# The length-1 step of a recurrent layer: gates as seven half-size products in place of eight

## The chip, the cores and the metric

The kernel runs on one core of a Trainium2 chip. The metric is device time in microseconds (us), the median over runs. Engines are named as in the profile: PE is TensorE's matmul, PEld its weight load, DVE is VectorE, ACT is ScalarE, POOL is GpSimd, SP is SyncE, which here issues DMAs. "L1368" is line 1368 of the kernel before. Each engine works through a queue of its own, in order, and waits on semaphores for the others.

## The reference

Four residual layers over `x` of 128 x 64 x 256, each followed by a layer norm. The change is in the fourth. It makes `h` with two graph convolutions and then runs four small LSTMs over `h`, with windows of 1, 2, 3 and 4 steps, each writing back the last step of each window:

```python
h = relu(einsum('ts,bsh->bth', adj, x @ Wg0 + bg0))
h = relu(einsum('ts,bsh->bth', adj, h @ Wg1 + bg1))
for p in range(1, MAX_SKIP + 1):
    nw = Tv // p
    wins = h[:, :nw * p, :].reshape(Bv * nw, p, Hd)
    last = lstm_last(Wih[p - 1], Whh[p - 1], bih[p - 1], bhh[p - 1], wins)
    idx = arange(nw) * p + (p - 1)
    h = h.at[:, idx, :].set(last.reshape(Bv, nw, Hd))
```

For a window of one step the state is zero, so the f gate and `Whh` drop out:

```python
i, g, o = sigmoid(x Wi + bi), tanh(x Wg + bg), sigmoid(x Wo + bo)
h = o * tanh(i * g)
```

Each of x Wi, x Wg, x Wo is a product of rows of 256 with a 256 x 256 matrix, in float32.

## The kernel before

The layer works on four pairs (`pair` 0 to 3) of 32 batches. `Hs[pair]` holds `h` transposed: 128 partitions of features, then two halves `n` of 16 batches, two feature blocks `k`, 64 time steps, 16 batches. The loop `lstm(pair)` runs lengths 1 to 4 one after another and yields after each unit of work; units 0 to 7 are length 1, 8 to 21 length 2, 22 to 32 length 3, 33 to 47 length 4. At those yields side steps are run, as `put(pair, part, *units)` has entered them by hand: `gcn` (the graph convolutions that make the next pair's `h`; eleven steps each: load, two fetches, two norms, neighbours, and so on), `final` (residual, norm and output of what is finished, in two steps), and `prepare` (load of a length's weights; at the first use also the sums of weight blocks on POOL, L1198).

Everything in the loop is issued through `given` (L110), which puts each instruction behind the latest one of PE, DVE, ACT and POOL, so that the order of an engine's queue is the order of the program. Waits come from the data: reading what was written, and overwriting what is still to be read, PSUM banks and SBUF tiles alike.

Length 1 before: for each half n and each run of 32 time steps (512 columns) and each output block j of 128, three gates i, g, o with two products each (L1368), so 8 units of 6 products, 48 in a pair. ACT evaluates each gate out of its PSUM bank (L1372), DVE multiplies i and g (L1373), ACT takes tanh (L1374), DVE multiplies by o into `h` (L1379). There are six banks for this ring (`lbank`).

Lengths 2 to 4 make their later steps with seven products of 128 x 128 blocks in place of eight (class `Gate`), with sums of weight blocks (`S`) and of input columns (`xsums`, `hsums`). Each product has a bank of its own. The class `Seven` of the third layer (L796) does the same in three banks and accumulates a second product into a bank that was copied out.

The weights of lengths 2 to 4 live in two rotating pairs of tiles, `wx` (8 x 512 per partition) and `wh` (7 x 512). The weights of length 3 take the tiles that length 4 of the pair before has used. Their load is step `prepare(weights_of[k, 3])` at unit 0.

Of the kernel before, what the change touches and what calls it, by code (L numbers as in the profile page):

```python
# [17 lines left out]
P = 128  # L18
NB = 128
N = 64  # L20
# [21 lines left out]
def kernel(ctx: ExitStack, tc: tile.TileContext, i, out):  # L42
# [1125 lines left out]
    class Weights:  # L1168
# [7 lines left out]
        def load(self):  # L1176

            x = we.tile([P, 8, 2 * D], F32, name="wx", bufs=2)
            h = we.tile([P, 7, 2 * D], F32, name="wh", bufs=2)
            self.tiles = x, h  # L1180
            raw = [t[:, :4].rearrange("p k c -> p (k c)").rearrange("p (k c) -> p k c", k=KD) for t in (x, h)]
            if self.p in self.ready:
                for t, d in zip(self.tiles, self.ready[self.p]):
                    nc.sync.dma_start(t, d)
            else:
                for t, w in zip(raw, (i["WihT"], i["WhhT"])):
                    nc.sync.dma_start(t, w[self.p - 1].rearrange("(k p) c -> p k c", p=P))
            self.raw = [t.rearrange("p k (g m c) -> p k g m c", g=4, m=2) for t in raw]
            sums = [[t[:, j].rearrange("p (g c) -> p g c", g=4) for j in range(4, t.shape[1])] for t in (x, h)]

            self.S = [sums[0], [self.raw[1][:, 0, :, 1]] + sums[1]]
# [156 lines left out]

    def lstm(pair):
# [4 lines left out]


        for n in range(2):
            for w0 in range(0, N, QT // GB):
                Hw = H[:, n, :, w0:w0 + QT // GB, :]
                ends = []

                def gates(j):
                    i_, g_ = (late.tile([P, QT // GB, GB], F32, name="gate", bufs=6) for _ in range(2))
                    o = late.tile([P, QT // GB, GB], F32, name=("hid", "hs")[j], bufs=1)
                    banks = [lbank([QT // GB, GB]) for _ in range(3)]
                    for b, name in zip(banks, "igo"):
                        mw = {"i": 0, "g": 2, "o": 4}[name] + j
                        for k in range(KD):
                            nc.tensor.matmul(b, wih1[:, k, mw * P:(mw + 1) * P], Hw[:, k],  # L1368
                                             start=k == 0, stop=k == KD - 1)
                    for b, name, dst in zip(banks, "igo", (i_, g_, o)):  # L1370
                        at, f = gate_of(name)
                        nc.scalar.activation(dst, b, f, bias=bias[:, 0, 2 * at + j:2 * at + j + 1])  # L1372
                    nc.vector.tensor_mul(i_, i_, g_)  # L1373
                    nc.scalar.activation(g_, i_, AF.Tanh)  # L1374
                    ends.append((o, g_))
                    if j == KD - 1:

                        for jj, (o, t) in enumerate(ends):
                            nc.vector.tensor_mul(Hw[:, jj], o, t)  # L1379

                for j in range(KD):
                    given(gates, j)
                    yield "at", unit
                    unit += 1

        for p in range(2, SKIP + 1):
# [80 lines left out]
            def late_columns(r):  # L1467

                if pair < NP - 1 or p == 2 or r:
                    return [slice(0, nw)], []  # L1470
                mine, q = range(nw), p - 1
                wrote = [w for w in mine if w * p % q == q - 1 and w * p < N // q * q and (q > 2 or w * p >= N // 2)]
                step = wrote[1] - wrote[0]
                assert wrote == list(range(wrote[0], nw, step))[:len(wrote)]
                if wrote[0] < step:
                    return [slice(n, nw, step) for n in range(step) if n != wrote[0]], [slice(wrote[0], nw, step)]
                return [slice(0, wrote[0])], [slice(wrote[0], nw)]

            def begin(n, r, ms, parts):
# [3 lines left out]
                for m in ms:  # L1483
                    if (n, m) not in begun:
                        begun[n, m] = lbank([2, nw, GB]) if joint else [lbank([nw, GB]) for g in range(2)]
                    for g in range(1 if joint else 2):
                        for c in parts:
                            for k in range(KD):
                                x = inp(r, 0, k)
                                b, x = (begun[n, m][:, :, c], x[:, :, c]) if joint else (begun[n, m][g][:, c], x[:, g, c])  # L1490
                                nc.tensor.matmul(b, w.raw[0][:, k, at, m, :], x, start=k == 0, stop=k == KD - 1)  # L1491
# [210 lines left out]
    first = [prepare(weights_of[0, p]) for p in (2, 3)]  # L1702
    for n in [0, 0, 0, 1, 1, 0, 1, 0, 0, 1, 0, 0, 1, 1, 0, 2, 1, 3, 1, 1, 2, 2, 3, 3]:
        given(next, parts[n])
    for part in first:
        next(part)
# [13 lines left out]
    put(0, first[1], 9, 11)  # L1720
# [7 lines left out]
    for k in range(NP):  # L1728
        if k:
            put(k, prepare(weights_of[k, 3]), 0)  # L1730
# [3 lines left out]
        for n in range(2):  # L1734
# [4 lines left out]
            if k < NP - 1:  # L1739
                put(k + 1, final(g, SKIP - 1), n, n + 2)  # L1740
        if k < NP - 1:
            put(k, prepare(weights_of[k + 1, 2]), 34)
            for n, keys in enumerate([
                    [0, 2, 3, 5, 6, 9, gap(11), 12, wait(15), 16, gap(18)],
                    [2, 5, 6, 8, 9, 19, wait(22), gap(22), gap(25), 26, gap(29)],
                    [6, 8, 9, 12, 13, 27, wait(33), gap(33), gap(36), 37, 38],
                    [9, 11, 12, 15, 16, 34, gap(40), 41, gap(44), 45, 46]]):
# [49 lines left out]
```

## Time and profile before

| what | us |
|---|---|
| median of three runs (2048.69 to 2051.10) | 2050.42 |
| profiled execution | 2053.11 |
| its span, first to last instruction | 2050.9 |
| length 1 of pair 0 (with the last steps of the first `h`) | 798.4 to 861.9 |
| length 1 of pair 1 | 1132.7 to 1173.9 |
| length 1 of pair 2, first and last start of a product | 1444.5 to 1485.3 |
| length 1 of pair 3, first and last start of a product | 1756.4 to 1797.1 |

In a group of instructions the columns are: line, engine, operation, output <- inputs, shapes, count, then busy us and mean ns of one, then idle time of the engine just before and who ended it. In a table of windows: the window, its length, busy us and instruction count of PE, PEld, DVE, ACT and POOL, the clock that was granted to PE (1.00 is full), the share of the DMA engines and GB/s. In a timeline: start, length, engine, line, operation, count of merged instructions, and in brackets the idle time before. A float32 product shows as two records.

### The profile page before, as it was taken

To read this page: it belongs to the slowest core of one execution; us is meant where nothing else is said; L and a number is where in the kernel's file an instruction comes from. 1 tells how busy PE (TensorE), PEld (TensorE's weight loads), DVE (VectorE), ACT (ScalarE), POOL (GpSimd) and SP (SyncE) were. 2 spreads that over 40 slices of the span, in tenths; PEclk is the share of its full clock that TensorE was granted. 3 is DMA by queue.
4 is the path that set the end of the run, shared out by engine and by line. 5 is a ranking of instruction groups with operands and counts; after the bars stand their busy time and mean duration, and the time that the engine had idled before them with its cause. 6 is when DMAs were issued, how large, how long until landed. Compare 5 with 4: busy or idle time off the path is not lost.

```text
span 2050.9 us, 31078 instructions
## 1 busy us (share of the span) xinstructions
PE 1959.1 (96%) x11391; PEld 1329.2 (65%) x11391; DVE 1185.8 (58%) x2683; ACT 968.4 (47%) x1852; POOL 809.7 (39%) x961
## 2 busy tenths in 40 slices
PE   5999999999899999999999999999999999999996
PEld 4666667766454445577678477677567667568685
DVE  7456665564457456574466674456674457544566
ACT  2766667666334633544343644343544333543333
POOL 1123334343345535263445253345243335224264
PEclk8999999999999998999999999999999999999998
DMA  5344442332112026351232532032532022401022
GB/s 137 74 66 68 79 69 54 66 49 40 31 35 60 26 97 242 124 180 52 88 139 63 185 114 93 11 128 72 169 101 83 1 109 70 141 0 77 1 65 69
DMA packets 235959, 170.66 MB, mean 83 GB/s; under 512 B 150560, under 2 KB 213536, under 8 KB 232480
## 3 DMA queue, kind: packets, MB, share of 16 engines
q1 hardware_dynamic: 233952, 166.72, 28.7%
q8 instruction: 90, 1.47, 0.3%
q0 software_dynamic: 1024, 1.05, 0.2%
q10 hardware_dynamic: 832, 0.92, 0.1%
q14 instruction: 61, 0.50, 0.1%
HBM read 107.82 MB, written 60.82 MB: 82 GB/s over the span
## 4 chain that ended last, share of the span: by engine, by line
PE 74%; DVE 13%; POOL 4%; ACT 4%; issue 3%; DMA 2%; SPq 1%; POOLq 0%; ACTq 0%; DVEq 0%
PE l L1535 27%; PE l L1491 9%; PE l L1368 8%; PE pz L820 4%; PE e L346 3%; PE pz L749 3%; PE m L318 3%; PE g L1331 2%; PE pz L1017 2%; PE m L321 2%; PE z L355 2%; PE m L253 2%; PE m L436 1%; PE g L1319 1%; DVE ln_st L95 1%
## 5 line engine op out<-in xcount | busy, mean ns | idle before, releaser
L1535 PE MATMUL l<-xs,wx 128*128 128x256 f32 (+1 forms) x896 | 276.8, 399 | 5.0 <-DVE gate L1554 4.0
L1535 PE MATMUL l<-hs,wh 128*128 128x256 f32 (+1 forms) x896 | 275.1, 399 | 3.1 <-DVE hs L1405 3.1
L86 POOL TENSOR_TENSOR ln_rs<-ln_rs,mhalf 128x2 f32<-128x2 f32 (+2 forms) x98 | 84.3, 860 | 448.9 <-DVE ln_rs L98 442.9
L1550 ACT ACTIVATE kept<-l 128x256 f32<-128x256 f32 (+1 forms) x224 | 88.6, 403 | 339.7 <-PE l L1535 338.4
L1535 PE MATMUL l<-H,wx 128*128 128x256 f32 (+1 forms) x672 | 210.2, 401 | 3.4 <-DVE gate L1563 3.4
L1535 PE MATMUL l<-hid,wh 128*128 128x256 f32 (+1 forms) x672 | 208.8, 399 | 0.0
L1535 PEld LDWEIGHTS l<-xs,wx 128*128 128x128 f32 x896 | 168.8, 190 | 49.3 <-POOL st L100 4.1
L1535 PEld LDWEIGHTS l<-hs,wh 128*128 128x128 f32 x896 | 169.3, 190 | 45.5 <-DVE hs L1405 5.7
L1568 ACT ACTIVATE gate<-gate,bias 128x512 f32<-128x512 f32 (+1 forms) x280 | 170.6, 657 | 37.4 <-DVE gate L1559 31.1
L1491 PE MATMUL l<-H,wx 128*128 128x512 f32 (+4 forms) x576 | 183.7, 475 | 2.2 <-DVE H L1441 2.2
L1368 PE MATMUL l<-H,wih 128*128 128x512 f32 x384 | 167.4, 596 | 0.0
L357 ACT ACTIVATE u<-z 128x1024 f32<-128x1024 f32 x128 | 130.4, 1025 | 64.3 <-PE z L355 63.2
L1535 PEld LDWEIGHTS l<-H,wx 128*128 128x128 f32 x672 | 125.9, 190 | 42.8 <-issue 7.4
L1491 PEld LDWEIGHTS l<-H,wx 128*128 128x128 f32 x576 | 100.9, 190 | 76.2 <-issue 53.6
L1535 PEld LDWEIGHTS l<-hid,wh 128*128 128x128 f32 x672 | 127.2, 190 | 32.0 <-issue 2.6
L1368 PEld LDWEIGHTS l<-H,wih 128*128 128x128 f32 x384 | 73.2, 191 | 90.1 <-issue 83.1
L1558 POOL TENSOR_TENSOR gate<-gate,kept 128x256 f32<-128x256 f32 (+1 forms) x84 | 65.2, 776 | 158.6 <-DVE kept L1556 158.6
L329 DVE TENSOR_TENSOR qs<-m,qs 64x256 fp32r<-64x256 f32 x128 | 54.0, 422 | 109.9 <-ACT qs L328 107.8
L1409 POOL TENSOR_TENSOR hs<-hid 128x256 f32<-128x256 f32 (+1 forms) x28 | 25.5, 909 | 192.3 <-DVE hid L1438 98.6
L355 PE MATMUL z<-gath_r,qs 128*128 128x512 f32 x256 | 100.8, 482 | 0.1
L1463 ACT ACTIVATE gate<-cell 128x512 f32<-128x512 f32 (+1 forms) x88 | 58.6, 666 | 81.7 <-DVE cell L1455 59.5
L1552 DVE TENSOR_TENSOR gate<-l,kept 128x256 f32<-128x256 f32 (+1 forms) x112 | 49.1, 438 | 72.0 <-ACT gate L1568 44.1
(336 smaller groups left out, 3825.9 us busy)
## 6 DMA issues: line engine op xcount, KB each, us to landing
wx<-sums SPq DMA_DIRECT2D x9, 2048.0 KB
wh<-sums SPq DMA_DIRECT2D x9, 1792.0 KB
way<-st SPq DMA_DIRECT2D x54, 256.0 KB
st<-way SPq DMA_DIRECT2D x216, 64.0 KB
xin<-in_x SPq DMA_DIRECT2D x16, 512.0 KB
ld<-table SPq DMA_DIRECT2D x16, 512.0 KB
x_dram<-y SPq DMA_DIRECT2D x16, 512.0 KB
x2r<-x_dram SPq DMA_DIRECT2D x32, 256.0 KB
```

Of the source, the lines that this page charges most:

```text
L86: nc.gpsimd.tensor_tensor(dst, dst, mhalf[:, :n], OP.pow)
L318: nc.tensor.matmul(pq, xT[:, k, c * P:(c + 1) * P], wq[:, k, :], start=k == 0, stop=k == KD - 1)
L346: nc.tensor.matmul(pes[S][n * CG:(n + 1) * CG, :], apad[:, k, CG - HEADS - r0:2 * CG - HEADS - r0], u[:, k, :], start=r0 == 0 and k == 0, ...
L355: nc.tensor.matmul(z[:, k, :], L1[q]["qs"][c][:, s, k * P:(k + 1) * P], gath_r, start=True, stop=True)
L357: nc.scalar.activation(u, z, AF.Relu)
L820: nc.tensor.matmul(self.bank[at], lhs, rhs, start=first and n == 0, stop=n == len(self.terms) - 1, skip_group_check=True)
L1368: nc.tensor.matmul(b, wih1[:, k, mw * P:(mw + 1) * P], Hw[:, k], start=k == 0, stop=k == KD - 1)
L1491: nc.tensor.matmul(b, w.raw[0][:, k, at, m, :], x, start=k == 0, stop=k == KD - 1)
L1535: nc.tensor.matmul(self.banks[j], lhs, rhs, start=src == 0, stop=src == 1)
L1550: nc.scalar.activation(self.keep(j), b, AF.Copy)
L1558: e.tensor_tensor(t[0][:, 1], t[0][:, 1], k[5], OP.add)
L1568: given(lambda: nc.scalar.activation(dst, dst, f, bias=b))
```

## The change

For each half n the three gates g, i, o are now made whole, in this order: 256 output rows in two blocks m, 1024 columns in two halves v of 512. Weight and input are cut into 2 x 2 blocks and the product is made with seven block products (`Wide`, `seven`) in three banks: products 1 and 2 share one, 6, 7 and 4 another, 5 and 3 the third. ACT copies products 1 and 5 out, DVE adds 6, 3, 7 and 4 to what has been kept, POOL makes one more sum; the gate's functions then work in place, three of four out of SBUF. Product 4 and most of a gate's functions and multiplies (`tail`) are issued between the products of the next gate. The first g of each pair, and in pair 0 both g, are still made with eight products (`eight`).

The sums of input columns (`column_sums`, four POOL operations of 512 for each n) and the sums of weights (`Sx`), two buffers for copies (`firsts`) and half of i's result (`spare`) lie in the tiles of the weights of length 3, which `room` reserves and `load` fills later. The weight sums are computed once (`first_sums`, POOL, ahead of pair 0), stored, and fetched by DMA in later pairs. `column_sums(1)` is issued at the start of n=1 in pair 0, and after gate i of n=0 in the others.

Length 2 begins with products of half n=0 alone for g and, in part, i (`late_columns`, `begin`), ahead of those of n=1.

Side steps: the load of length 3's weights goes from unit 0 to 8 (pair 0: load 8, sums 13 and 15, from a load ahead of the loop and sums at 9 and 11); the last finals from n and n+2 to 9+n and 12+n; the loads, fetches and norms of three of the four `gcn` parts to later units. The numbering of units is kept: g, i, o of n=0 are units 0, 1, 2, unit 3 follows at once; likewise 4 to 7.

```diff
+    def first_sums():
+        S = rooms_of(0)[1]
...
+        for dst, x, y, op in ((2, a11, a21, OP.subtract), (0, a21, a22, OP.add), (1, S[:, 0], a11, OP.subtract),
+                              (3, a12, S[:, 1], OP.subtract)):
+            nc.gpsimd.tensor_tensor(S[:, dst], x, y, op)
+        d = dram.tile([P, 3 * QT], F32, name="sums1")
+        nc.sync.dma_start(d, S.rearrange("p j g c -> p (j g c)"))
+        sums_kept.append(d)
...
+        Tn, Sx, firsts, spare = rooms_of(pair)
+        if pair:
+            nc.sync.dma_start(Sx.rearrange("p j g c -> p (j g c)"), sums_kept[0])
...
+        def column_sums(n):
+            T, e = Tn[n], nc.gpsimd
+            e.tensor_tensor(T[:, 0], half(n, 0, 1), half(n, 0, 0), OP.subtract)
+            e.tensor_tensor(T[:, 1], half(n, 1, 1), T[:, 0], OP.subtract)
+            e.tensor_tensor(T[:, 2], half(n, 1, 1), half(n, 0, 1), OP.subtract)
+            e.tensor_tensor(T[:, 3], half(n, 1, 0), T[:, 1], OP.subtract)
...
+            def product(self, j):
+                b = given(self.multiply, j)
+                t, add = self.t, nc.vector.tensor_add
+                if j == 1:
+                    given(nc.scalar.activation, self.first, b, AF.Copy)
+                elif j == 5:
+                    given(nc.scalar.activation, t[1][1], b, AF.Copy)
+                elif j == 2:
+                    self.act(0, 0, b)
+                elif j == 6:
+                    given(add, t[0][1], b, self.first)
+                elif j == 3:
+                    given(add, t[0][1], b, t[0][1])
+                elif j == 7:
+                    given(add, t[1][0], b, self.first)
+                    given(nc.gpsimd.tensor_tensor, t[1][1], t[1][0], t[1][1], OP.add)
+                else:
+                    given(add, t[1][0], b, self.first)
...
+            def after(self, m, v):
+                if self.name == "i":
+                    g = self.gates["g"][m][v]
+                    if m:
+                        given(nc.gpsimd.tensor_tensor, self.t[m][v], self.t[m][v], g, OP.mult)
+                    else:
+                        given(nc.vector.tensor_mul, self.t[m][v], self.t[m][v], g)
+                    given(nc.scalar.activation, self.t[m][v], self.t[m][v], AF.Tanh)
+                elif self.name == "o":
+                    given(nc.vector.tensor_mul, half(self.n, m, v), self.t[m][v], self.gates["i"][m][v])
+
+            def tail(self):
+                self.act(0, 1)
+                yield
+                self.after(0, 0)
+                self.after(0, 1)
+                yield
+                self.product(4)
+                self.act(1, 1)
+                yield
+                self.act(1, 0)
+                yield
+                self.after(1, 1)
+                self.after(1, 0)
+
+            def last(self):
+                self.act(0, 1)
+                self.product(4)
+                self.after(0, 0)
+                self.act(1, 0)
+                self.after(1, 0)
+                self.act(1, 1)
+                self.after(0, 1)
+                self.after(1, 1)
...
+        def seven(G, rest, order):
+            G.product(order[0])
+            next(rest, None)
+            G.product(order[1])
+            next(rest, None)
+            G.product(order[2])
+            next(rest, None)
+            G.product(order[3])
+            next(rest, None)
+            for _ in rest:
+                pass
+            for j in order[4:]:
+                G.product(j)
+
+        rest = iter(())
         for n in range(2):
...
+            if n == 0:
+                given(column_sums, 0)
+            elif pair == 0:
+                given(column_sums, 1)
+            gates = {}
+            for name in "gio":
+                G = Wide(name, n, gates)
+                if name == "g" and (n == 0 or pair == 0):
+                    eight(G, rest)
+                    rest = iter(())
+                else:
+                    seven(G, rest, (1, 6, 5, 2, 7, 3) if (n, name) == (1, "o") else (1, 6, 5, 2, 3, 7))
+                    rest = G.tail()
+                if (n, name) == (1, "o"):
+                    G.last()
+                elif name == "i" and n == 0 and pair:
+                    given(column_sums, 1)
+                yield "at", unit
+                unit += 1
+            yield "at", unit
+            unit += 1
...
+                if p == 2 and r == 0:
+                    return [(slice(0, 1), every)], [(slice(1, 2), every)]
...
-    for part in first:
-        next(part)
+    given(first_sums)
+    next(first[0])
...
-    put(0, first[1], 9, 11)
+    put(0, first[1], 8, 13, 15)
...
-            put(k, prepare(weights_of[k, 3]), 0)
+            put(k, prepare(weights_of[k, 3]), 8)
...
-                put(k + 1, final(g, SKIP - 1), n, n + 2)
+                put(k + 1, final(g, SKIP - 1), 9 + n, 12 + n)
...
-                    [0, 2, 3, 5, 6, 9, gap(11), 12, wait(15), 16, gap(18)],
-                    [2, 5, 6, 8, 9, 19, wait(22), gap(22), gap(25), 26, gap(29)],
-                    [6, 8, 9, 12, 13, 27, wait(33), gap(33), gap(36), 37, 38],
-                    [9, 11, 12, 15, 16, 34, gap(40), 41, gap(44), 45, 46]]):
+                    [0, 1, 3, 5, 7, 9, gap(11), 12, wait(15), 16, gap(18)],
+                    [5, 9, 11, 13, 15, 19, wait(22), gap(22), gap(25), 26, gap(29)],
+                    [13, 17, 19, 21, 23, 27, wait(33), gap(33), gap(36), 37, 38],
+                    [21, 24, 26, 28, 30, 34, gap(40), 41, gap(44), 45, 46]]):
```

## The prediction

> Forecast: **slower by about 7.6 us**. The profiled execution took 2053.1 us (span 2050.9 and 2.2 around it) and would become 2060.7; the median shown, 2050.4, lies 2.7 below that execution, and I move it by the same sum: **2058.0 us**. About 0.2%, 4.1 us, is what can be told from no change.
>
> **What bounds the kernel now.** First the page's busy line, then windows over the stages of length 1 (one for each of four pairs), then TensorE's lines in order of time.
>
> ```profile
> PE 1959.1 (96%) x11391; PEld 1329.2 (65%) x11391; DVE 1185.8 (58%) x2683; ACT 968.4 (47%) x1852; POOL 809.7 (39%) x961
> ...
> 798.00:862.00 64.00, 62.20 (x406) 32.60 (x405) 33.70 (x72) 29.71 (x47) 24.65 (x29) 0.97 0.42 149
> ...
> 1132.50:1174.00 41.50, 41.50 (x99) 18.52 (x98) 24.64 (x59) 24.72 (x42) 9.96 (x15) 1.00 0.59 198
> ...
> L1368 PE MATMUL l<-H,wih 128*128 128x512 f32 x384 | 167.4, 596 | 0.0
> ...
> 1132.71 41.36 PE L1368 MATMUL l<-H,wih 128*128 128x512 f32 x96
> ```
>
> In the second pair's stage PE is busy for 41.50 of 41.50 us with nothing but L1368. A product is two records, so 384 records are 192 products: 167.4/192 = 0.872 us each, and 48 of them are the 41.4 us run. The other three engines have room. So products removed are time won, and every wait that PE newly has is time lost. In pair 0 the last norms of the first H run beside the stage:
>
> ```profile
> 806.88 1.10 POOL L100 TENSOR_SCALAR A<-x2r,ln_rs 128x256 f32<-128x256 f32 x2
> 807.94 5.18 POOL L1198 TENSOR_TENSOR wx<-wx 128x512 f32<-128x512 f32 x4
> 813.08 6.50 POOL L1198 TENSOR_TENSOR wh<-wh 128x512 f32<-128x512 f32 x4
> ...
> 807.50 1.24 PE L1249 MATMUL l<-bdT,A 64*64 64x64 f32 x32 [1.43 <-POOL A L100]
> 808.67 6.70 PE L1368 MATMUL l<-H,wih 128*128 128x512 f32 x12
> ...
> 815.01 1.76 DVE L1379 TENSOR_TENSOR H<-hid,gate 128x512 f32<-128x512 f32 x1
> 816.70 1.75 DVE L1379 TENSOR_TENSOR H<-hs,gate 128x512 f32<-128x512 f32 x1
> 818.37 1.27 DVE L1321 TENSOR_TENSOR hT<-g,rb 128x512 f32<-128x512 f32 x2
> ...
> 808.00:810.00 2.00, 1.97 (x18) 1.33 (x19) 0.69 (x1) 0.60 (x1) 2.00 (x2) 0.50 0.30 98
> ```
>
> Two things to see: POOL is occupied until 808.0, and after PE's gaps there its clock is 0.50 and six products take 6.70 us where they take 5.3.
>
> **The skill.** The Trainium skill (GPSIMD Engine Reference, 1. Specifications) says that GpSimd shares its SBUF interfaces with VectorE and contends with DVE instructions that have two SBUF inputs. The rows above agree: L1379 (two SBUF inputs) takes 1.76 beside L1198 where it takes 0.69 elsewhere, and the four POOL sums 6.50 instead of 5.18; L1321, with one input from PSUM, keeps its 0.64 each. I take 1.76 for such a multiply, and 0.65 more on POOL for each. Second, TensorE: Matmul & The Clock Gate (Part 1) puts the slow clock after an idle window of about 3.4 us. Here it came after less (0.52 us busy of 806 to 808). I go by the trace: 1.4 us lost after such a gap.
>
> **Prices.** From rows of this trace, end to end: ACT gate from PSUM 0.69 (L1372), Copy from PSUM 0.60 (L830), gate in place 0.66 (L1568), tanh 0.63 (L1374); the next one starts about 0.1 before such an end. DVE add with one PSUM input 0.69 (L832), two-SBUF multiply 0.69 alone. POOL sum of 128x512 1.27 (L116). A product can be read about 0.17 after its issue slot (its records last 0.59, issued every 0.44).
>
> **What is removed.** Per pair there are six gates (two halves n; g, i, o) of eight products. Seven of eight are made in four gates of pair 0 and five of each later pair: 19 products, 19 x 0.872 = **-16.6 us** (3.5, 4.4, 4.4, 4.4).
>
> **Pairs 1 to 3, start.** First g is eight products, 7.0 us. Beside it POOL makes the column sums, four times 1.27, and the 0.79 MB of weight sums comes by DMA; wx<-sums moves 350 to 390 GB/s, so some 2.3 us and about 2 us to start. Product 6 of i needs them at 7.9. Hidden by 2 us or more; nothing charged.
>
> **Gate o of n=0 and g of n=1.** Clock: o's product 1 starts at 0; PE's order is 1, 6, 5, i's 4, 2, 3, 7, each 0.87. ACT's order is copy 1, i's act, tanh, tanh, copy 5, i's act, o's act, i's act, tanh, tanh: ten operations, about 6.1 us, in a gate of 6.1 us. Product 3 accumulates into the bank of product 5, so it waits for copy 5, and that stands behind two tanhs whose multiplies stand on DVE behind the add of product 6.
> - Add 6: 1.95 to 2.6. POOL has i's last add 0.9 to 2.2, then column_sums(1), so both multiplies contend: to 4.3 and 5.95. Second tanh to 6.6, copy 5 to 7.15. Product 3 would have started at 4.36: wait **2.8**.
> - The other two multiplies of i are on POOL behind column_sums(1): sums 5.16 plus 1.3 of contention end at 8.6, multiplies at 9.9 and 11.2, last tanh 11.85. In pairs 1 and 2 the two scales of the moved fetch (unit 3) follow, 1.0; then copy 1 of g, to 13.35. g's product 2, which needs that bank, would start at 8.9+3.5 = 12.4: wait **1.0**, and product 3 waits **0.2** for its copy. In pair 3 (no fetch) copy 1 ends at 12.35: 0.0 and 0.2.
> - Sum 4.0 in pairs 1 and 2, 3.0 in pair 3. Contention moves waits between the two gates more than it changes the sum: without any it is about 2.5 and 1.6.
>
> **Gate i of n=1**: ACT has six operations; no wait.
>
> **Gate o of n=1.** Unit 5 puts a norm (DVE 1.9 us, as at 1165.4 to 1167.3) ahead of its add 6 in pairs 0 to 2. Copy 5 then ends at 5.7; product 3 is last here and due at 5.2: **0.5**. Pair 3: 0.
>
> **End of stage.** Before, length 2 began with windows that the last unit did not write, so PE had no wait (L1491 follows at once). Now its first products need the half just written. Covers: the g and i products of half n=0, six of 0.43 = 2.6 us. The chain: i's last two POOL multiplies end about 8.2 after o's start, tanh 8.85, act 9.4, act 10.0, multiply 10.7; PE has products until 7.0 and cover to 9.6: **1.15**, with the norm 1.35.
>
> **Pair 0.** first_sums (four sums of 384 elements, about 1.0 each between the 336-wide at 0.90 and the 512-wide at 1.27) queue on POOL behind the norms, 808.0 to 812.0; the first two column sums end at 814.6. PE: g to 805.4, the neighbour products to 808.5 (waiting about 0.9 for POOL, as before), i's product 1 to 809.4, product 6 waits to 814.6: **5.2**, and the clock gap **1.4**. o of n=0, with no column sums beside it: **0.8** to 1.0. Then g of n=1 follows the H writes of the parts directly (before, six products of n=0 stood between: PE 836.24, H written to 837.4): **1.2**. o and the end: 0.5 and 1.35. New waits 10.6 with the 0.9 that stay about 11.5; before, this stage lost 1.8 to waits and 1.4 to the clock. 11.5 - 3.2 - 3.5 = **+4.8**.
>
> **Moved steps.** Length-3 weights go from unit 0 to 8 (their 3.8 MB kept the queues over 0.8 busy from 1133 to 1148; first needed at unit 22), so SP's queue is freer early; finals to 9 to 13, norms and fetches to 9 to 30, with their way DMAs behind that load but three units ahead of their use. Finals at 12 and 13 add DVE blocks of 2.6 us to a stage with PE waits of 2.6 us in all, per pair, over lengths 2 to 4. Bounds -2 and +2 per pair; I take 0. The halved beginning of length 2 makes twice the records at half the columns: 0. A tanh that comes first could need another table load, 1.28 (L1372's), hidden in g: 0.
>
> **Sum.** Pair 0 +4.8; pairs 1 and 2: 4.0+0.5+1.35 = 5.85 less 4.36, +1.5 each; pair 3: 3.0+1.15 less 4.36, -0.2. Total **+7.6**.
>
> **Rivals.**
> - *The waits just eat the gain*, within 0.2%: there is no contention and the fetch's scales run earlier (o and g of pairs 1 to 3 at 2.5, 2.5 and 1.6: -4.4) and the pair 0 wait is 2 to 3 us shorter. +1, 2051. For: ACT is free before o. Against: the 1.76 rows.
> - *Faster*: PE does not wait for the chain from POOL's multiplies through tanh to ACT's copies. It decides at copy 1 of g ending before 9.6 after o's start (mine: 13.35). Then the waits of o and g go in all pairs (4.0, 4.0, 3.0, 0.8: -4.2 in all), and those at the ends, which stand behind the same multiplies, too (5.2): -9.4, 2041. For: POOL is busy for 24% of the stage before. Against: POOL takes its queue in order, and the program puts the column sums first.
> - *More than forecast*: each wait over 2 us also drops the clock, 1.4 in three pairs, and the DVE blocks of unit 12 and 13 cost their bound, 4 over pairs 1 and 2: +16, 2066. For: the 0.50 clock after a short gap. Against: 1.2 us waits late in the kernel left it at 1.00.
>
> **Numbers.** Forecast 0.53, within 0.2% 0.21, faster 0.16, more than forecast 0.10. Faster 0.16, same 0.21, slower 0.63. The likeliest case's own range is 2054.5 to 2063; the range 2045 to 2067 leaves out most of the faster case and the outer part of the last.
>
> **What would show it.** 43 or 44 products of 512 in each stage. PE waits for an ACT copy at product 3 of each o of n=0 and, in pairs 1 and 2, at product 2 of the next g; for POOL column sums once, about 5 us, near 809; for the H multiply at the start of length 2, about 1.2 us each. Stages of about 43 us in pairs 1 and 2, against 41.5. Wrong if PE stays at 100% there, if the wait near 809 is missing, or if lengths 2 to 4 change by more than 2 us per pair.

## The result and the profile after

The changed kernel takes 2067.28 us, median of four runs (2063.85 to 2069.47), against 2050.62 for the kernel before (2048.69 to 2051.10): a ratio of 1.0082, interval 1.0064 to 1.0099. It is slower by 16.7 us where 7.6 were forecast, and 0.3 us beyond the top of the range. The sign, the places of the new waits and most of their lengths came as forecast; their sum did not.

The profiled execution took 2069.47 us (span 2067.7), 2.2 above its median. The one shown of before was 2.5 above this median, and at least that much lies ahead of length 1: its first product of length 1 starts at 798.4, that of the trace after at 793.7, and its clock was 0.90 in the first 100 us, where the trace after has 0.93. From the first product of length 1 to the end of the span, where none of that counts, the two traces have 1252.5 and 1274.0 us. So the forecast's +7.6 stands against +21.5 of this one execution. By stages, from the start times of the products:

| stage | before | after | difference |
|---|---|---|---|
| pair 0, length 1 | 63.7 | 70.2 | +6.5 |
| pair 0, length 2 | 83.1 | 86.6 | +3.5 |
| pair 1, length 1 | 41.2 | 42.2 | +1.0 |
| pair 1, length 2 | 83.1 | 85.3 | +2.2 |
| pair 2, lengths 1 and 2 | 124.3 | 126.8 | +2.5 |
| pair 3, length 1 to the start of length 3 | 110.1 | 114.5 | +4.4 |
| length 3 of pairs 0, 1 and 2 | 262.3 | 264.0 | +1.7 |
| all the rest | 484.7 | 484.4 | -0.3 |

The page's busy line, and those rows of TensorE's waits of the changed kernel that the kernel before does not have (waited for; us in total, times, longest us). L1437 is a product of the seven, L1500 of the eight, L1659 the first step of length 2, L116 the helper through which `Wide` issues its functions, sums and multiplies.

```profile
PE 1950.8 (94%) x11449; PEld 1338.6 (65%) x11449; DVE 1236.3 (60%) x2743; ACT 987.1 (48%) x1890; POOL 902.0 (44%) x1032
...
PE l L1437 <- ACT gate L116: 10.6, 7, 2.5
PE l L1437 <- POOL wx L1392: 6.2, 1, 6.2
PE l L1659 <- DVE H L116: 5.9, 8, 1.2
PE l L1500 <- ACT H L1348: 1.3, 1, 1.3
PE l L1703 <- ACT gate L1673: 0.8, 1, 0.8
PE l L1437 <- ACT wh L116: 0.5, 1, 0.5
```

By the page TensorE is busy for 8.3 us less, but 6.1 of that lie ahead of length 1. From the first product of length 1 on it is busy for 2.2 us less (1221.2 for 1223.3), where 19 products fewer are worth 19 x 0.858 = 16.3 (a product starts every 41.2/48 = 0.858 us in a full stream of the kernel before; the prediction's 0.872 has the half clock of pair 0 and the ends of its runs of products in it). So 14 us of the saving are gone in busy time: products at half clock are longer, and so, as shown further down, are the products beside a wait. The other three engines carry 50, 19 and 92 us more. TensorE has 25.3 us of waits that it did not have, and 1.6 fewer behind POOL in pair 0: 25.3 - 1.6 - 2.2 = 21.5. The timelines show where. Pair 0 first:

```profile
803.24 1.12 PE L1437 MATMUL l<-H,wih 128*128 128x512 f32 x2
810.57 3.78 PE L1437 MATMUL l<-wx,wh 128*128 128x512 f32 x4 [6.20 <-POOL wx L1392]
814.14 1.92 PE L1437 MATMUL l<-H,wih 128*128 128x512 f32 x2
815.84 1.44 PE L1437 MATMUL l<-H,wh 128*128 128x512 f32 x2
...
831.11 1.13 PE L1437 MATMUL l<-H,wh 128*128 128x512 f32 x2 [1.80 <-ACT gate L116]
```

Then gate o of n=0 in pair 1, its end of stage, the same gate in pair 2, and the start of length 2 in pair 3:

```profile
1154.35 1.02 PE L1437 MATMUL l<-H,wih 128*128 128x512 f32 x2
1157.87 1.97 PE L1437 MATMUL l<-H,wh 128*128 128x512 f32 x2 [2.50 <-ACT gate L116]
1159.64 1.92 PE L1437 MATMUL l<-wx,wh 128*128 128x512 f32 x2
1161.34 1.07 PE L1437 MATMUL l<-H,wih 128*128 128x512 f32 x2
...
1179.16 1.13 PE L1437 MATMUL l<-H,wh 128*128 128x512 f32 x2 [0.45 <-ACT gate L116]
...
1184.91 0.70 PE L1659 MATMUL l<-H,wx 128*128 128x256 f32 x2 [1.17 <-DVE H L116]
...
1469.91 1.02 PE L1437 MATMUL l<-H,wih 128*128 128x512 f32 x2
1473.43 1.13 PE L1437 MATMUL l<-H,wh 128*128 128x512 f32 x2 [2.50 <-ACT gate L116]
1474.39 1.02 PE L1437 MATMUL l<-wx,wh 128*128 128x512 f32 x2
1475.25 1.02 PE L1437 MATMUL l<-H,wih 128*128 128x512 f32 x2
...
1814.50 0.70 PE L1659 MATMUL l<-H,wx 128*128 128x256 f32 x2 [1.01 <-DVE H L116]
1815.86 6.49 PE L1659 MATMUL l<-H,wx 128*128 128x256 f32 x21 [0.65 <-DVE H L116]
```

Product 3 of o waits 2.50 for the copy of product 5 in each of pairs 1 to 3 (forecast 2.8), product 3 of the last o waits 0.45 in pairs 0 to 2 (0.5), and at the start of length 2 TensorE waits 1.17 and 0.24 in pairs 0 to 2 (1.35 in all) and 1.01 and 0.65 in pair 3 (1.15). The first of the surprises is beside it. Products 3 and 7 take 1.97 and 1.92 in pair 1 and 1.13 and 1.02 in pair 2 after the very same wait of 2.50. The windows show a different clock (columns as in the tables of windows before: the clock granted is the third number from the end); the last two rows are pair 2's:

```profile
810.00:812.00 2.00, 1.44 (x2) 0.84 (x3) 0.00 (x0) 0.00 (x0) 1.78 (x2) 0.50 0.94 351
1158.00:1160.00 2.00, 2.00 (x3) 0.94 (x4) 0.12 (x1) 1.61 (x3) 2.00 (x2) 0.50 0.00 0
1790.00:1792.00 2.00, 2.00 (x3) 0.67 (x2) 0.69 (x2) 0.71 (x2) 2.00 (x3) 0.50 0.00 0
1818.00:1820.00 2.00, 2.00 (x6) 1.56 (x6) 0.00 (x0) 1.03 (x2) 0.82 (x2) 0.50 0.78 186
...
1472.00:1474.00 2.00, 0.57 (x2) 0.34 (x3) 0.83 (x2) 1.74 (x4) 1.92 (x2) 1.00 0.22 65
1474.00:1476.00 2.00, 2.00 (x6) 0.91 (x5) 1.24 (x2) 1.21 (x3) 2.00 (x3) 1.00 0.00 0
```

The clock was halved within the long wait of pair 0 and behind the wait in pairs 1 and 3, and once more at the start of length 2 in pair 3, behind the waits of 1.01 and 0.65. In pair 2 it was not.

### The profile page after: what moved, and what is told of

Same layout as the page of the kernel before. It is cut to its first block, busy times and chain, and to the rows that moved or that the text cites. A ratio compares the mean times of both kernels' runs of the same rounds, so it can differ in the third digit from the quotient of the medians.

```text
span 2067.7 us, 31491 instructions
## 1 busy us (share of the span) xinstructions
PE 1950.8 (94%) x11449; PEld 1338.6 (65%) x11449; DVE 1236.3 (60%) x2743; ACT 987.1 (48%) x1890; POOL 902.0 (44%) x1032
## 3 DMA queue, kind: packets, MB, share of 16 engines
q0 software_dynamic: 1024, 1.05, 0.2%
## 4 chain that ended last, share of the span: by engine, by line
PE 67%; DVE 16%; POOL 6%; ACT 5%; issue 3%; DMA 1%; SPq 1%; DVEq 0%; ACTq 0%; POOLq 0%
PE l L1703 26%; PE l L1659 8%; PE pz L820 4%; PE l L1437 4%; PE pz L749 3%; PE e L346 2%; PE m L318 2%; PE g L1336 2%; PE pz L1017 2%; PE m L321 2%; PE z L355 2%; DVE ln_st L95 2%; PE m L253 1%; PE g L1324 1%; PE l L1500 1%
## 5 line engine op out<-in xcount | busy, mean ns | idle before, releaser
L1659 PE MATMUL l<-H,wx 128*128 128x256 f32 (+5 forms) x672 | 187.8, 435 | 8.5 <-DVE H L116 5.9
L1659 PEld LDWEIGHTS l<-H,wx 128*128 128x128 f32 x672 | 119.7, 192 | 70.7 <-issue 34.4
L1703 PEld LDWEIGHTS l<-H,wx 128*128 128x128 f32 x672 | 125.8, 190 | 42.5 <-DVE gate L1731 7.4
L1613 POOL TENSOR_TENSOR cell<-gate,cell 128x512 f32<-128x512 f32 (+1 forms) x56 | 75.5, 1368 | 28.4 <-ACT gate L1736 28.4
L1731 DVE TENSOR_TENSOR gate<-l,gate 128x256 f32<-128x256 f32 (+1 forms) x112 | 50.0, 446 | 61.4 <-POOL gate L1726 35.1
```

Source lines behind the costliest of these rows:

```text
L1613: nc.gpsimd.tensor_tensor(c, t, c, OP.mult)
L1703: nc.tensor.matmul(self.banks[j], lhs, rhs, start=src == 0, stop=src == 1)
```

## The experiments

Four kernels take one cause each out of the changed kernel, one puts the moved steps alone into the kernel before, two join the repairs, one tests an order on POOL. Each was timed beside the kernel before, on the same chip.

**The weight sums of pair 0.** They are issued ahead of the last four steps of the first norms (`at` counts these steps):

```diff
...
+        if at == 20:
+            given(first_sums)
         given(next, parts[n])
-    given(first_sums)
```

> The weight sums are issued on POOL ahead of the last four norms of the first H instead of behind them; nothing else is moved. Theory A (the order of POOL's queue makes the 6.2 us wait of PE before product 6 of i in pair 0, and that gap halves PE's clock for some 5 us, a loss of about 3): the column sums start when the norms end (802.8 in the changed kernel) in place of 806.8, so the wait shrinks from 6.2 to about 2.3, and the clock loss from 3 to between 0 and 1.5; in all 5.5 to 7 us less, a median of about 2061. Theory B (the wait is for something else, such as the memory of the tiles or H): the wait stays and less than 1 us is won. If only the gap counts and the slow clock has another cause, 3.9 are won.

Measured 2063.42 us (2061.98 to 2064.61), ratio 1.0058 (1.0042 to 1.0075).

```profile
PE l L1437 <- POOL wx L1392: 2.1, 1, 2.1
```

The wait falls from 6.2 to 2.1, and the stage from 70.2 to 64.9. By the ratios about 5 us are won, somewhat less than the 5.5 to 7 expected, and the intervals of the two kernels overlap: it is the trace that decides. So it was the queue on POOL (norms, weight sums, column sums, in that order), as the prediction had it.

**The column sums of n=1, in pairs 1 to 3.**

```diff
             if n == 0:
                 given(column_sums, 0)
+                if pair:
+                    given(column_sums, 1)
...
-                elif name == "i" and n == 0 and pair:
-                    given(column_sums, 1)
```

> In pairs 1 to 3 the column sums of n=1 are issued right behind those of n=0, at the start of the stage, so that they are off POOL before gate o of n=0. Theory A (in these pairs the wait before product 3 of o and the one before product 2 of g come from POOL's column sums: they contend with DVE's two multiplies and stand ahead of POOL's multiplies): the 2.5 us wait before product 3 falls to about 0.7, there is no wait and no slow clock behind it; 3.6, 2.7 and 3.6 us less in the three pairs, about 10 in all, a median of about 2057. Theory B (ACT's queue of ten operations sets both waits, contention moves nothing): the wait stays above 2 us and less than 2 us are won in all. The waits of about 1.4 at the start of length 2 stay in both.

Measured 2059.65 us (2058.97 to 2062.33), ratio 1.0045 (1.0029 to 1.0062): by the ratios 7.6 us, the largest single repair, where about 10 were expected.

```profile
PE l L1437 <- ACT gate L116: 5.0, 7, 1.8
```

The 2.50 us waits are gone from all three pairs, and the clock stays at 1.00 there; lengths 1 and 2 gain 3.1, 2.5 and 5.3 us. The chain behind the waits can be read on the engines in pair 1 of the changed kernel, which are VectorE's two multiplies of i, POOL's column sums beside them, and the copy on ScalarE that comes last:

```profile
1153.51 3.16 DVE L116 TENSOR_TENSOR cell<-cell,hid 128x512 f32<-128x512 f32 x2
...
1154.41 1.71 POOL L1393 TENSOR_TENSOR wx<-H 128x512 f32<-128x512 f32 x1
1156.08 1.72 POOL L1392 TENSOR_TENSOR wx<-H,wx 128x512 f32<-128x512 f32 x1
...
1156.70 0.63 ACT L116 ACTIVATE cell<-cell 128x512 f32<-128x512 f32 x1 [1.05 <-DVE cell L116]
1157.24 0.58 ACT L116 ACTIVATE gate<-l 128x512 f32<-128x512 f32 x1
```

Two multiplies of two SBUF inputs take 3.16 beside the sums. Alone, two take 1.28 in this trace. The second tanh waits for them, the copy of product 5 (`gate<-l`) stands behind the tanh in ScalarE's queue, and product 3 waits for the copy.

**The copies ahead of i's tanhs.**

```diff
                 self.act(0, 1)
                 yield
-                self.after(0, 0)
-                self.after(0, 1)
                 yield
                 self.product(4)
                 self.act(1, 1)
                 yield
                 self.act(1, 0)
+                self.after(0, 0)
+                self.after(0, 1)
```

> In the tail the first two multiplies and tanhs of i come behind the functions of the second row block, so that ACT's copy of product 5 no longer stands behind them. Theory A: in pair 0 the waits before product 3 of o go (1.8 and 0.45 us), in pairs 1 and 2 that of the second o (0.45); in pairs 1 to 3 the 2.5 us wait before product 3 of the first o goes too, but a wait of 2.7 to 3.7 us comes before product 2 of the following g, since the chain of POOL's sums and multiplies up to the last tanh is as long as before: nothing won there but the place of the wait. The waits at the start of length 2 shrink by up to 1.4 each, since the functions of i come earlier. In all 5 to 8 us less, a median of 2059 to 2062. Theory B (ACT's order alone is the cause): no wait is left between o and g, 13 us or more won, a median under 2054.

Measured 2065.98 us (2065.76 to 2066.63), ratio 1.0073 (1.0056 to 1.0090).

```profile
PE l L1437 <- ACT wh L116: 9.4, 4, 3.2
PE l L1437 <- DVE gate L116: 5.1, 4, 1.4
```

By the ratios about 2 us are won, where 5 to 8 were expected, and the intervals overlap. The wait went from product 3 of o to product 2 of the next g, and grew to 3.15 in pairs 1 and 2: that product needs a bank that ScalarE copies out behind the same tanhs, which still stand behind the column sums. A second wait is new and was not foreseen. In n=1 product 4 of o comes behind VectorE's add of product 7, which is queued behind the two moved multiplies, 1.4 in pairs 0 to 2 and 1.0 in pair 3. What came as expected is the start of length 2, which has no wait behind the H multiplies any more in any pair; in pair 1:

```profile
1181.56 1.12 PE L1437 MATMUL l<-wx,wih 128*128 128x512 f32 x2 [1.37 <-DVE gate L116]
1182.52 7.22 PE L1659 MATMUL l<-H,wx 128*128 128x256 f32 x32
```

Length 2 of pairs 0 to 2 takes 84.8, 83.5 and 83.5, where the changed kernel has 86.6, 85.3 and 85.4. Most of that wait has moved ahead of product 4: lengths 1 and 2 of pair 2 together take 125.8 for 126.8. An order on one engine's queue is not free to choose for one consumer.

**The last sum on VectorE.**

```diff
-                    given(nc.gpsimd.tensor_tensor, t[1][1], t[1][0], t[1][1], OP.add)
+                    e = nc.vector if (self.n, self.name) == (1, "o") else nc.gpsimd
+                    given(e.tensor_tensor, t[1][1], t[1][0], t[1][1], OP.add)
```

> The one POOL add of the last gate of a stage (o of n=1) is made by DVE. In the changed kernel DVE's add of product 4 overwrites what POOL's add reads, and waits 2.55 us for it; POOL makes it behind two multiplies of i. Theory A (that wait sets when the last multiply of H comes): the last needed H comes about 0.9 earlier, the wait of PE at the start of length 2 falls from about 1.4 to 0.5 in every pair, with the slow clock behind it in pair 3; 4 to 5 us less, a median of about 2063. Theory B (the tanh behind POOL's multiplies and ACT's functions behind it set it): less than 1 us in all.

Measured 2064.99 us (2061.75 to 2066.19), ratio 1.0069 (1.0052 to 1.0086). The interval overlaps that of the changed kernel, so the time alone says little. The reason to try it was this row of the changed kernel, VectorE's add of product 4 of the last o:

```profile
1183.57 0.69 DVE L116 TENSOR_TENSOR gate<-l,wh 128x512 f32<-128x512 f32 x1 [2.55 <-POOL gate L116]
```

It overwrites what POOL's sum still has to read, and POOL has i's two multiplies ahead of it. The prediction had the multiplies but not this overwriting. With the sum on VectorE the start of length 2 waits 1.1 once in each pair in place of 1.2 and 0.2; the chain through i's multiplies, tanh and the last functions stays about as long. A quarter of the wait, then, not the whole.

**The moved side steps alone, in the kernel before.** The lists of units behind `gcn` are those of the change too (left out here):

```diff
-    put(0, first[1], 9, 11)
+    put(0, first[1], 8, 13, 15)
...
-            put(k, prepare(weights_of[k, 3]), 0)
+            put(k, prepare(weights_of[k, 3]), 8)
...
-                put(k + 1, final(g, SKIP - 1), n, n + 2)
+                put(k + 1, final(g, SKIP - 1), 9 + n, 12 + n)
...
```

> The kernel before (length 1 with eight products) with nothing of the change but the moved side steps: length 3's load at unit 8, the last finals at 9+n and 12+n, and the loads, fetches and norms of the graph convolutions at the units of the change. Theory A (the moved steps are a small part of the loss): length 2 of pair 0 grows by 0.85 to 1.3 us, because two steps of sums and the second norms now lie beside it, length 3 of the four pairs by 0.45 to 0.8 us each, length 1 stays at 41.2 us per pair; 1 to 4 us over the kernel before in all, 2052 to 2055. Theory B (the moved steps carry most of the loss, and the waits in length 1 only took back the saving): 7 us or more over the kernel before, 2058. Theory C (my forecast's figure): within 1 us of the kernel before.

Measured 2052.44 us (12 runs, 2051.04 to 2054.59) beside 2050.19 for the kernel before (31 runs), ratio 1.0010 (1.0001 to 1.0019): about 2 us. The stages show it: length 2 of pair 0 takes 84.4 (83.1 before), length 3 of pairs 0 and 1 takes 87.9 and 88.3 (87.4), length 1 and length 2 of pairs 1 and 2 and length 3 of pair 2 are unchanged. In pair 0 one wait is new:

```profile
913.18 1.28 PE L1535 MATMUL l<-H,wx 128*128 128x256 f32 x4 [0.85 <-ACT gate L1505]
```

**The repairs together.** The edits of the four kernels, with that of the tanhs for n=0 alone, and for pair 0 gate i of n=0 in an order that needs the column sums one product later, and one norm of the graph convolution a unit earlier (4 in place of 5):

```diff
-                    seven(G, rest, (1, 6, 5, 2, 7, 3) if (n, name) == (1, "o") else (1, 6, 5, 2, 3, 7))
+                    seven(G, rest, (1, 6, 5, 2, 7, 3) if (n, name) == (1, "o") else
+                          (1, 2, 5, 6, 3, 7) if (pair, n, name) == (0, 0, "i") else (1, 6, 5, 2, 3, 7))
...
-                    [0, 1, 3, 5, 7, 9, gap(11), 12, wait(15), 16, gap(18)],
+                    [0, 1, 3, 4, 7, 9, gap(11), 12, wait(15), 16, gap(18)],
```

> The changed kernel with the repairs together: weight sums ahead of the last four norm steps of the first h; column_sums(1) behind column_sums(0) in pairs 1 to 3; the two tanhs of i's first block moved behind the two evaluations of i's second block, for n=0 alone; the last sum of gate o of n=1 made by VectorE; and, in pair 0, gate i of n=0 in the order 1, 2, 5, 6, 3, 7 and one norm of the graph convolution one unit earlier. Theory A (the waits are separate losses, so that their gains add): about 6 us (weight sums), 11 us (column sums), 2 to 5 us (the last sum) and 1 to 3 us (tanhs and order) below the changed kernel; length 1 takes 64 us in pair 0, 37 to 38 in pairs 1 to 3; 2040 to 2046, below the kernel before by 4 to 10 us. Theory B (TensorE then waits for the next engine in the same places, since VectorE and ScalarE carry more in a shorter stage): the gains overlap, and the time is 2050 or more, no less than the kernel before.

Measured 2048.18 us (20 runs, 2043.51 to 2050.39) beside 2050.19, ratio 0.9989 (0.9982 to 0.9996): 2 us below the kernel before, short of the expected 4 to 10. Nothing speaks against gains that add: the four ratios fall below the changed kernel's by 0.24%, 0.37%, 0.09% and 0.13%, 0.83% or 17 us together, and the joint kernel, with the order and the norm besides, by 0.93%; each single ratio is known to about 0.17%. The amounts that I had written down were read off single traces, of which the changed kernel's was its slowest run. Length 1 came as expected, 63.7 in pair 0 and 37.9 in pair 1 (41.2 before). What is left is in these rows:

```profile
PE l L1665 <- DVE H L116: 4.4, 4, 1.1
PE l L1437 <- ACT wh L116: 2.0, 4, 0.9
PE l L1437 <- DVE cell L116: 1.3, 1, 1.3
```

Length 2 still starts 1.1 late in each pair (84.8 in pair 1, 83.1 before), and gate i of n=1 in pair 0 waits twice.

**The last gate with eight products.** As the joint repairs, but gate o of n=1 is made by `eight`, which then issues o's multiplies itself, two of them ahead of the rest of i and two behind it; there is no sum of o left to move; i's second block of n=1 is multiplied on VectorE in place of POOL; and in pair 0 the norm is back at unit 5:

```diff
-                if name == "g" and (n == 0 or pair == 0):
+                if name == "g" and (n == 0 or pair == 0) or (n, name) == (1, "o"):
                     eight(G, rest)
...
-                    if m:
+                    if m and not self.n:
                         given(nc.gpsimd.tensor_tensor, self.t[m][v], self.t[m][v], g, OP.mult)
...
-                if (n, name) == (1, "o"):
-                    G.last()
...
```

> As e6_all_four, with gate o of n=1 made by eight products whose sums ScalarE reads straight from their banks (no copies, no sums on VectorE or POOL behind the last product), i's second block of n=1 multiplied on VectorE, and, for pair 0, the norm of the graph convolution back at unit 5. Theory A (the wait of 1.1 us at the start of length 2, and the stop in PE's work around it, come from the chain of copies, sums and POOL work behind the last product of o, and the waits of 0.9 and 1.3 us in gate i of n=1 of pair 0 from the norm put ahead of its first sum): the wait at the start of length 2 falls below 0.3 us in each pair, length 1 grows by 0.86 us a pair and length 2 shrinks by 1.3 to 1.6, and pair 0 gains 2 to 3: 3 to 6 us below e6_all_four, 2042 to 2045. Theory B (the wait comes from the write of H itself, the last gate function and two multiplies, whatever makes the gate): the wait stays at 0.8 us or more, and with four more products the time is 2048 or more but for pair 0's 2 us.

Measured 2041.06 us (2039.18 to 2042.35) beside 2048.75 for the kernel before on that chip, ratio 0.9961 (0.9947 to 0.9975). It is faster than both kernels, by 0.39% or 8 us against the kernel before, and against the joint repairs by 0.28% or 5.7 us. First the end of the stage in pair 1, then, from pair 0, VectorE's two multiplies into H and ScalarE's copy of product 5 behind them, and TensorE's product 3:

```profile
1165.78 1.88 PE L1504 MATMUL l<-H,wih 128*128 128x512 f32 x4
1167.49 7.45 PE L1668 MATMUL l<-H,wx 128*128 128x256 f32 x32
...
844.16 2.35 DVE L116 TENSOR_TENSOR H<-gate,wh 128x512 f32<-128x512 f32 x2
...
846.00 0.60 ACT L116 ACTIVATE wh<-l 128x512 f32<-128x512 f32 x1 [1.85 <-DVE H L116]
...
846.65 1.12 PE L1437 MATMUL l<-H,wh 128*128 128x512 f32 x2 [0.89 <-ACT wh L116]
```

Length 2 now starts without a wait. Length 1 of pair 1 grew from 37.9 to 38.6 and length 2 fell from 84.8 to 83.6: one product more in each stage is cheaper than the chain of copies, sums and multiplies behind the last product. Which of the three, the plain products, the multiplies off POOL or the order of o's multiplies, takes the wait away was not separated. Pair 0's length 1 falls from 63.7 to 61.1, but some 1.7 of that is a stretch of half clock (850.2 to 853.6 in the trace of the joint repairs) that this trace does not have. Of the two waits in pair 0 the one of 1.3 has gone with the norm's old place. The other, 0.9, is still there, so the norm was not its cause: the copy of product 5 goes into `spare`, which o's multiplies of n=0 still read, and a pair of those takes 2.35 us there, beside sums of weights on POOL (840.7 to 845.4).

**The column sums in order.** Each of the four is issued by itself:

```diff
-            e.tensor_tensor(T[:, 0], half(n, 0, 1), half(n, 0, 0), OP.subtract)
+            given(e.tensor_tensor, T[:, 0], half(n, 0, 1), half(n, 0, 0), OP.subtract)
...
```

> The changed kernel with the four column sums issued one by one, so that POOL makes them in the order 0, 1, 2, 3 (in the changed kernel the third of the text, which needs nothing but H, runs before the second). Theory A (1.0 to 1.3 us of the wait of 6.2 us in pair 0 is the sum that runs ahead of the one that product 6 reads): that wait becomes 4.9 to 5.2, the rest stays. Theory B (product 6 waits for something else, or the order does not matter): 6.0 to 6.3. The wait of 2.5 us at gates g of pairs 1 to 3 stays as it is, whether or not the clock falls behind it; the whole is 1 to 2 us below the changed kernel.

Measured 2063.77 us (2060.70 and 2066.84), ratio 1.0072 (1.0052 to 1.0092).

```profile
PE l L1437 <- ACT gate L116: 10.7, 7, 2.5
...
PE l L1437 <- POOL wx L116: 5.1, 1, 5.1
...
1153.80 1.13 PE L1437 MATMUL l<-H,wh 128*128 128x512 f32 x2 [2.50 <-ACT gate L116]
1154.77 1.02 PE L1437 MATMUL l<-wx,wh 128*128 128x512 f32 x2
```

The wait is 5.1, where the prediction had 5.2. (With two runs the time itself tells nothing: its interval overlaps that of the changed kernel.) `given` keeps the order between calls, and in the changed kernel all four sums are one call, within which the third was put ahead of the second. The expectation's "gates g" is a slip: the waits of 2.5 are those of gate o of n=0. They are as long as in the changed kernel, and this time the clock stayed at 1.00 behind all three.

## Why the prediction was right or wrong

**Right: direction, places, and most waits.** Product 6 in pair 0, product 3 of both o, the H multiply at the start of length 2, the first g of n=1 in pair 0 behind H (1.28, forecast 1.2), contention of VectorE's multiplies with POOL (1.58 each here, 1.76 forecast) and the extra on POOL (0.45 each on two sums, 0.65 forecast) all came. The rival "faster" fell by its own test: the tanh ahead of copy 1 of g in pair 1 ended at 1162.2, 11.3 us after o's start (forecast 11.85), so the copy was not through before 9.6. Stages of about 43 us were forecast for pairs 1 and 2, and 42.2 and 41.5 came. The rival "the waits just eat the gain" needed no contention, and contention there was.

**Wrong: the sum.** One of the prediction's own signs of being wrong came too: lengths 2 to 4 were to change by at most 2 us a pair, and lengths 2 and 3 of pair 0 grew by 4.3. In the traces 13.9 us are missing between +7.6 and +21.5. By the prediction's own steps:

- *"The clock gap 1.4", charged once, in pair 0.* This is the largest term. In the profiled execution the four products from 810.57 to 817.12 take 6.55 in place of 3.43 (3.1 lost); products 3 and 7 in pair 1 take 3.47 where they take 1.82 in pair 2 (1.7 lost); five products in pair 3 take 6.09 for 4.29 (1.7 more than pair 2's 0.1), and 21 records at the start of length 2 there take 6.49, where 18 take 4.15 in pair 2 and so 21 would take 4.8 (1.7). 8.2 in all, where the trace of before had 1.4: 6.8 more than the forecast. It was in the rival "more than forecast", as 1.4 in three pairs after waits over 2 us. The size and the places are about right, but how often it falls is a draw: the wait of 2.50 in gate o occurs twelve times in the traces of the changed kernel and of the kernels with early weight sums, with the sum on VectorE and with ordered sums, and the clock fell behind three of them. What is drawn is said below.
- *"1.15, with the norm 1.35" for the start of length 2.* The prediction counts a wait from the slot in which the product was due. Counted so, the products of n=0 and n=1 at the start of length 2 take 8.95 to the next neighbour products in pairs 0 to 2, where the kernel before takes 6.96: 2.0 lost in each. In pair 3 it is 2.2 beside the clock. That is 3.0 more in all. The neighbour products behind them then take 1.3 in place of 1.1: 0.6 more over three pairs, which no experiment here explains.
- *"Moved steps ... I take 0", with bounds of ±2 for each pair.* About 2 us in time for all four, as the kernel with the moved steps alone showed; 2.6 by the stages of its trace. Only pair 0's length 2, with two steps of sums added, reaches 1.3.
- *"The first two column sums end at 814.6".* The sum that product 6 reads was the third on POOL: 1.1 us, shown by ordering the sums. Product 6 started 6.5 us after it was due, where 5.2 were forecast: 1.3 more.
- *"o of n=0 [of pair 0]: 0.8 to 1.0".* It lost 2.1: 1.2 more.
- *The last o, 0.5 in three pairs.* It lost 0.7 in each: 0.6 more. The first g of n=1 in pair 0 lost 0.1 more than its 1.2.
- *"g's product 2 ... wait 1.0, and product 3 waits 0.2" in pairs 1 and 2, and 0.2 in pair 3.* Together they lost 1.0 in pair 2 and nothing in pairs 1 and 3, where the half-clock products came between: 1.6 less. The neighbour products of pair 0 did not wait for POOL any more: 0.9 less. Product 3 of o in pairs 1 to 3 lost 2.76 each where 2.8 were forecast: 0.1 less.
- *"19 x 0.872".* 0.858 by the run of 48 products: 0.3 less saved.

6.8 + 3.0 + 0.6 + 2.6 + 1.3 + 1.2 + 0.6 + 0.1 - 1.6 - 0.9 - 0.1 + 0.3 = 13.9, against 13.9. So close a sum is luck in part: in pairs 1 to 3 such terms meet the measured stages within 0.2 us, in pair 0 they come out 0.6 too high. Three steps failed above all: the half clock, charged once at 1.4 where it came four times and took 8.2; the start of length 2, where 2.0 to 2.2 were lost and not 1.15 to 1.35; and the moved steps, put at nothing.

The idle time that the profile shows is less than what a wait costs. In pair 2, where the clock stayed up, from product 2 of o (1469.91) to product 7 (1474.39) are 4.48 us: two slots of 0.86, 2.50 of idle, and 0.26 more. The rows say where these are: product 2 is busy for 1.02, though in a full stream the next starts 0.86 after it, so 0.16 pass before the idle time begins; and product 3, the first behind the wait, takes 0.96 to the next start, 0.10 more than a slot.

The comparison of medians is kinder than that of the traces, because the trace of before had lost time early and the trace after was one with much half clock: 16.7 against 7.6. The four runs of the changed kernel fall in the order of their mean granted clock: 0.981, 0.982, 0.983 and 0.985 for 2069.47, 2068.34, 2066.22 and 2063.85 us.

**What is drawn.** In each of the ten traces the granted clock is 1.00 or 0.50 and changes only on a grid of 3.413 us: of 141 changes between 50 and 2040 us none lies more than 0.0014 us off its trace's grid. The grid starts elsewhere in each trace, so it falls differently on the same wait. Here are the windows of the changed kernel's grid that hold the wait of 2.50 in pair 1, in pair 2 (two of them) and in pair 3:

```profile
1154.60:1158.01 3.41, 0.91 (x3) 0.14 (x2) 2.67 (x3) 1.94 (x4) 3.33 (x3) 1.00 0.27 77
...
1468.62:1472.03 3.41, 2.31 (x6) 0.76 (x4) 3.41 (x3) 0.75 (x2) 3.41 (x4) 1.00 0.34 116
1472.03:1475.44 3.41, 2.01 (x5) 1.06 (x6) 1.49 (x3) 2.91 (x5) 3.33 (x3) 1.00 0.13 38
...
1786.07:1789.48 3.41, 1.33 (x3) 0.68 (x4) 1.65 (x3) 2.50 (x5) 3.33 (x4) 1.00 0.00 0
```

In pair 1 TensorE is idle for 2.50 us of one window and in pair 3 for 2.08, and the next window has half clock. In pair 2 the grid cuts the wait into 1.10 and 1.40, and the clock stays. Of the twelve waits the three behind which the clock fell are those with 2.08 or more in one window; the others have 1.94 or less. Over all windows at full clock from 100 us on in the ten traces, half clock followed 44 of 44 with 2.0 us of idle time or more, 18 of 34 with 1.5 to 2.0, and none of 2283 with less.

The Trainium skill (TensorE: Matmul & The Clock Gate, Part 1) puts the slow clock after an idle window of about 3.4 us. The prediction went by the trace against it, rightly as to gaps: 2.0 us of idle time in a window were enough, in one wait or in two. What agrees with the page is the length of the window, 3.41 us here. In pair 1 the clock was at half from 1158.0 to 1161.4, one such window, and half of that, 1.7 us, is what it cost; in pair 0 it was at half for three, from 806.4 to 816.7, in part while TensorE was idle.

## What to carry to other kernels

Where one engine is full, products saved on it are worth what the engines behind it can keep up with: follow each product's bank to the engine that frees it, and that engine's queue to the slowest thing ahead. A scheme with fewer products and longer chains belongs in the middle of a stage rather than at its end: with the queues put in order and the last gate in the plain form the change became a gain of 8 us. Charge a wait of TensorE its idle time and about 0.3 us, and keep in the range 1.7 us for the clock wherever waits can leave TensorE idle for 1.5 us or more within 3.4 us.

## What the runs showed of the hardware

- The granted clock changed only on a grid of 3.413 us (141 changes in ten traces), and it went with TensorE's idle time within one window of that grid: half clock in the next window followed 2.0 us or more in 44 of 44 cases, 1.5 to 2.0 in 18 of 34, and less in none of 2283. So it followed the wait of 2.50 3 times in 12, two waits of 0.88 and 1.26 once together (in the joint repairs: 2.04 in one window), and the wait of 1.80 in pair 0 never in five traces.
- Half clock came in lengths of 3.41, 6.83 and 10.24 us in the stages of length 1, one, two or three windows, and one window cost a busy TensorE 1.7 us.
- A wait of TensorE in a stream of 128x512 float32 products cost 0.26 us beside the idle time shown: 0.16 of overlap lost behind the product ahead of it and 0.10 in the first product behind it.
- A 128x512 float32 multiply on VectorE with two SBUF inputs takes 0.64 to 0.69 alone and 1.58 beside a POOL sum of two inputs; the POOL sum goes from 1.26 to 1.71. VectorE's adds with one input from PSUM kept 0.69.
